# Two attention layers: every other step of the second layer in three products, its exponentials kept in PSUM and its differences taken on GpSimd

## The chip, the cores and the metric

The kernel runs on one core of one Trainium2 chip. The metric is the device time in microseconds (us) of one execution. The kernel before took 3224.03 us as the median of three runs (3221.72 to 3226.51). The execution that was profiled took 3222.18 us, with a span of 3220.4 us from its first to its last instruction. PE is TensorE, DVE VectorE, ACT ScalarE, POOL GpSimd and SP SyncE.

## The reference, cut to what matters

Two attention layers run one after the other on x of shape (4, 64, 64, 256) in fp32: 4 batches of 4096 tokens with 256 channels. A query or key has 32 channels; a value has 256 in the first layer and 128 in the second.

```python
# layer 0
q, k, v = x @ Wq + bq, x @ Wk + bk, x @ Wv + bv
attn = softmax(einsum('bnd,bmd->bnm', q, k), axis=-1)
x = gamma * einsum('bnm,bmc->bnc', attn, v) + x
# layer 1
f, g, v = x @ Wf + bf, x @ Wg + bg, x @ Wh + bh
beta = softmax(einsum('bqd,bkd->bqk', g, f), axis=-1)
x = x + (einsum('bqk,bkd->bqd', beta, v) @ Wo + bo)
```

## The kernel before, in words

No maximum is subtracted in the softmax: `fast_path` takes exp of the raw scores, and a slower general path runs only where sums or values leave a safe range. What is described here is `fast_path`.

**Tiling.** A step (`Step`, line 489) multiplies 1024 exponentials per partition with values. In the first layer (l = 0) a step covers 512 keys for 256 queries, with 8 steps per query block and 16 query blocks per batch. In the second layer (l = 1) a step covers 256 keys for 512 queries, with 16 steps per query block and 8 query blocks per batch. The loop over `steps` (line 654) runs batch by batch, first layer and then second.

**Precision.** In the trace a TensorE matmul of fp32 stands as two records and one of the rounded type fp32r as one. A product of two fp32 matrices can be put together from three fp32r products: rounded parts "high" of both, "low" of both, and differences "d" of both. That is a *split* step: six fp32r matmuls of 512 columns in the second layer. A *plain* step is two fp32 matmuls of 512 columns. Before, all first-layer steps are split, and of the 16 steps of a second-layer block three (i = 2, 7, 12; line 248).

**A step's work.** `scores` (line 498) is issued two steps ahead of the products: TensorE writes the 1024 scores into the PSUM tile `st` (two banks, one buffer). ScalarE reads them and writes exp, as `p`; in a split step it writes exp with a slightly lower bias, rounded, as `high` before it. `cut_low` (line 519), one step ahead, takes low = p - high on VectorE. `cut_both` (line 524) takes d from low and high on VectorE. `products_second` (line 544) adds to two accumulators in PSUM, one bank each, in the order high, low, d. VectorE adds every `p` of the second layer into `p_sum` (line 698), which gives the softmax's denominator.

**Side work.** Between the steps stand *units*: projections of the tokens of the next layer or batch (`project_units`, line 405: transposes, q and k in fp32r parts, v), in blocks of 512 tokens spread over a query block's steps (lines 700 to 705), and the ends of the query block before: `end_first` (line 566) and `end_second` (line 607: evacuate the accumulators, multiply by Wo, divide by the sums, add the residual, store).

**Memory.** [...] `st` 2, accumulators 4 (`ps_acc`), side work 2. In the second layer two of the accumulator banks belong to the current block and two to the one before. GpSimd has small additions (lines 593 and 676) and issues the loads of q and k (line 472), four per block.

**Order.** The source order is not that of the engines: the framework sorts the instructions[...].

## Time and profile before

| what | us or share | where from |
|---|---|---|
| span of the profiled execution | 3220.4 | page |
| time of the profiled execution | 3222.18 | times |
| median of the runs | 3224.03 | times |
| TensorE busy (granted clock 0.998) | 3166.5 (98%) | page |
| VectorE busy | 2691.5 (84%) | page |
| ScalarE busy | 1988.8 (62%) | page |
| GpSimd busy | 661.3 (21%) | page |
| idle before TensorE's matmuls, whole span | 45.9 | sum over the trace |
| layer 1 of batches 0, 1, 2: first to last product | 340.8 | trace, 518.5 to 859.3 and so on |
| layer 1 of batch 3, with no next batch to project for | 301.8 | trace, 2903.1 to 3204.9 |
| a second-layer query block, batches 0 to 2 | 41.7 | trace, starts of consecutive blocks |
| a second-layer query block, batch 3 | 37.2 | trace, 3013.3 to 3050.5 |

A matmul's duration in the trace [...]overlaps the next one's, so sums of durations exceed the time; the pitch is read from consecutive starts. An fp32 matmul of 512 columns stands as two records.

### The profile page before, as it was taken

Reading aid. Unit: us, or ns where it says so; the run is one execution under the profiler, and the core shown is the slowest. Engines: PE = TensorE matmul, PEld = TensorE weight load, DVE = VectorE, ACT = ScalarE, POOL = GpSimd, SP = SyncE. Lnnn points to the kernel's source line nnn. Section 1 sums busy time; section 2 is a strip of 40 time slices with the busy share of each in tenths; the row PEclk is TensorE's granted clock in tenths of the full one; section 3 lists DMA queues with packets and bytes.
Section 4 is the critical chain, followed back from the end, with each engine's and each line's share of the span. In section 5 each row is a group of like instructions: output and inputs, shape, how many; then the busy total and the mean of one; then the engine's idle time right before and its main releaser. Section 6 shows DMA issues by size and latency. Waiting matters only on the chain. (4 is left out here: it accounts for less than half of the span.)

```text
span 3220.4 us, 51144 instructions
## 1 busy us (share of the span) xinstructions
PE 3166.5 (98%) x19460; PEld 2613.0 (81%) x19460; DVE 2691.5 (84%) x3181; ACT 1988.8 (62%) x2483; POOL 661.3 (21%) x784
## 2 busy tenths in 40 slices
PE   8999999999999999999999999999999999999998
PEld 7999997566799999655679999966558999995554
DVE  7888888888888888788888888878888888887776
ACT  6666666655566666565556666655555666665554
POOL 3222223000232222200022222310002222241000
PEclk9999999999999999999999999999999999999999
DMA  4111123221212112322121112232222211121110
GB/s 120 47 47 44 50 50 83 56 53 49 59 44 54 44 52 49 79 53 53 49 64 42 49 50 50 61 70 52 51 52 57 53 41 47 46 70 47 36 36 31
DMA packets 368653, 172.16 MB, mean 53 GB/s; under 512 B 257392, under 2 KB 343664, under 8 KB 368400
## 3 DMA queue, kind: packets, MB, share of 16 engines
q1 hardware_dynamic: 342528, 134.29, 16.0%
q0 software_dynamic: 24960, 34.18, 4.5%
q8 instruction: 157, 2.57, 0.3%
q14 instruction: 96, 0.79, 0.1%
q10 hardware_dynamic: 912, 0.33, 0.0%
HBM read 99.22 MB, written 67.11 MB: 52 GB/s over the span
## 5 line engine op out<-in xcount | busy, mean ns | idle before, releaser
L517 ACT ACTIVATE p<-st 128x1024 f32<-128x1024 f32 x1024 | 1044.5, 1020 | 393.6 <-PE st L505 369.5
L515 ACT ACTIVATE high<-st,down 128x1024 fp32r<-128x1024 f32 x608 | 678.8, 1116 | 683.6 <-PE st L505 572.7
L527 DVE SCALAR_TENSOR_TENSOR d<-low,high 128x1024 fp32r<-128x1024 f32 x608 | 761.2, 1252 | 208.3 <-PE acc L536 202.9
L522 DVE TENSOR_TENSOR low<-p,high 128x1024 fp32r<-128x1024 f32 x608 | 810.6, 1333 | 134.2 <-ACT p L517 134.2
L557 PE MATMUL acc<-p,v 128*128 128x512 f32 x1664 | 795.2, 597 | 0.0
L505 PE MATMUL st<-q,k 128*128 128x256 f32 (+1 forms) x3072 | 778.6, 361 | 8.4 <-ACT p L517 8.3
L698 DVE TENSOR_TENSOR p_sum<-p_sum,p 128x1024 f32<-128x1024 f32 x480 | 587.1, 1223 | 60.7 <-ACT p L517 47.5
L505 PEld LDWEIGHTS st<-q,k 128*128 128x128 f32 x3072 | 461.2, 189 | 210.7 <-ACT p L517 113.3
L536 PE MATMUL acc<-v0d,d 128*128 128x258 f32 x4096 | 591.7, 284 | 1.7 <-DVE d L527 1.6
L536 PE MATMUL acc<-v0h,high 128*128 128x258 f32 x4096 | 588.6, 283 | 1.6 <-ACT high L515 1.6
L536 PE MATMUL acc<-v0l,low 128*128 128x258 f32 x4096 | 587.0, 283 | 0.5 <-DVE low L522 0.5
L536 PEld LDWEIGHTS acc<-v0d,d 128*128 128x128 f32 x4096 | 533.1, 189 | 6.7 <-DVE d L527 3.6
L536 PEld LDWEIGHTS acc<-v0h,high 128*128 128x128 f32 x4096 | 534.1, 190 | 3.4 <-ACT high L515 2.0
L536 PEld LDWEIGHTS acc<-v0l,low 128*128 128x128 f32 x4096 | 532.7, 189 | 0.8 <-DVE low L522 0.7
L557 PEld LDWEIGHTS acc<-p,v 128*128 128x128 f32 x1664 | 308.4, 190 | 214.3 <-issue 184.7
L593 POOL TENSOR_TENSOR x_res<-x,bo 128x256 f32<-128x256 f32 x128 | 216.3, 1690 | 889.9 <-DVE g L583 482.0
L472 POOL DMA_DIRECT2D q<-qk_dram x252 | 123.9, 501 | 1166.1 <-PE st L505 1143.0
L676 POOL TENSOR_TENSOR x_res<-x_res,bv 128x256 f32<-128x256 f32 x128 | 189.6, 1482 | 114.4 <-DMA x_res<-in_x 85.0
L442 PE MATMUL psv<-wv,xT 128*128 128x128 f32 (+1 forms) x1024 | 194.8, 331 | 6.8 <-DVE qk L423 6.1
L442 PEld LDWEIGHTS psv<-wv,xT 128*128 128x128 f32 x1024 | 159.6, 192 | 29.8 <-DVE qk L423 8.5
L472 POOL DMA_DIRECT2D k<-qk_dram x224 | 109.6, 500 | 245.2 <-PE st L505 140.3
L388 DVE TENSOR_TENSOR xl<-xT,xh 128x512 fp32r<-128x512 f32 x128 | 87.1, 683 | 5.1 <-ACT xh L387 4.7
(96 smaller groups left out, 1701.9 us busy)
## 6 DMA issues: line engine op xcount, KB each, us to landing
x_res<-in_x SPq DMA_DIRECT2D x128, 128.0 KB, 2.2
qk_dram<-qk_parts SPq DMA_DIRECT2D x64, 256.0 KB, 2.1
x_dram<-x SPq DMA_DIRECT2D x128, 128.0 KB, 1.7
x_res<-x_res SPq DMA_DIRECT2D x128, 128.0 KB, 1.7
squares<-x_dram SPq DMA_DIRECT2D x256, 64.0 KB, 2.3
x_old<-x_res SPq DMA_DIRECT2D x128, 128.0 KB, 2.0
out<-x_old SPq DMA_DIRECT2D x128, 128.0 KB, 1.7
q<-qk_dram POOLq DMA_DIRECT2D x252, 64.0 KB, 2.1
```

The costliest lines, as they stand in the source:

```text
L442: nc.tensor.matmul(ps[:, t, :], xT[key][:, c, (t0 + t) * P : (t0 + t + 1) * P], wv[l][:, c, :], start=(c == 0), stop=(c == NCC - 1),)
L472: nc.gpsimd.dma_start(dst[n * D : (n + 1) * D, :], parts[h, which])
L505: nc.tensor.matmul(st[:, g, :], k_t[b, l, kt // NT][:, kt % NT * P : (kt % NT + 1) * P], q_t[b, l, j * n // QB][:, q0 : q0 + n], start=Tru ...
L515: nc.scalar.activation(self.high, s_flat, AF.Exp, bias=down)
L517: nc.scalar.activation(self.p, s_flat, AF.Exp)
L522: nc.vector.tensor_sub(self.low, self.p, self.high.bitcast(F32))
L527: nc.vector.scalar_tensor_tensor(self.d, self.low.bitcast(F32), -1.0 / EPS, self.high.bitcast(F32), ALU.mult, ALU.add)
L536: nc.tensor.matmul(acc[2 * s + which][:, :W], p[:, g * QB0 + s * P : g * QB0 + (s + 1) * P], v0[self.i][v][:, g, :], start=self.first and ...
L557: nc.tensor.matmul(acc[which], v[:, g, :], p[:, g * QB : (g + 1) * QB], start=first and g == 0, stop=last and g == G[1] - 1,)
L593: nc.gpsimd.tensor_add(x_old[s], x_new[s], bo_sb)
L676: nc.gpsimd.tensor_add(x_res[b, j][t], x_res[b, j][t], bv)
L698: nc.vector.tensor_add(p_sum, p_sum, s.p)
```

## The change

Eight of the 16 steps of a second-layer block are split (all odd i), where three were. In such a step p is not written to SBUF: ScalarE overwrites the scores in PSUM with it. `high` is scaled down by 2^12 through its bias, so that low = p - 2^12 high is one VectorE instruction with one operand in PSUM and one in SBUF, and d = high - low is taken on GpSimd. Values and Wo are scaled to fit. `p_sum` is divided: VectorE adds the split steps and i = 4, 8, 12; GpSimd adds i = 0, 2, 6, 10, 14 into a second sum of 512 columns, in halves, and one more VectorE addition joins them.

PSUM's accumulators become two pairs of banks. In the second layer the pair that is not accumulating holds scores: steps i = 0, 1, 4, 5, ... use `st`, steps 2, 3, 6, 7, ... the other pair. In step 0 of a block the scores of step 2 are issued after the products, since that pair is the accumulator of the block before. `p` has two buffers instead of three.

Projections go in half blocks of 256 tokens at fixed steps (`plan`): of the next batch one half every 7 steps (transposes at step n, q and k at n + 2, v at n + 3), of the second layer one half per first-layer block.

```diff
+SPLIT1 = (1, 3, 5, 7, 9, 11, 13, 15)
+POOL_SUMS = (0, 2, 6, 10, 14)
...
-    split = [[l == 0 or i % 5 == 2 for i in range(NI[l])] for l in range(2)]
+    NH = N // QB0
+    split = [[l == 0 or i in SPLIT1 for i in range(NI[l])] for l in range(2)]
...
-    ps_st = ctx.enter_context(tc.tile_pool(name="ps_st", bufs=1, space=bass.MemoryType.PSUM))
-    ps_acc = ctx.enter_context(tc.tile_pool(name="ps_acc", bufs=4, space=bass.MemoryType.PSUM))
+    ps_main = ctx.enter_context(tc.tile_pool(name="ps_main", bufs=1, space=bass.MemoryType.PSUM))
...
-        return work.tile([P, 2 * QB], dtype, tag=tag, bufs={"d": 1, "p": 3}.get(tag, 2), name=name)
+        return work.tile([P, 2 * QB], dtype, tag=tag, bufs={"d": 1}.get(tag, 2), name=name)
...
-            st = ps_st.tile([P, G[l], n], F32, tag="st", name=f"st_{self.key}")
+            tag = "st" if l == 0 or i // 2 % 2 == 0 else f"pair{(j + 1) % 2}"
+            st = ps_main.tile([P, G[l], n], F32, tag=tag, name=f"st_{self.key}")
...
-                nc.scalar.activation(self.high, s_flat, AF.Exp, bias=down)
-            self.p = wide("t" if self.split and l == 1 else "p", f"p_{self.key}")
+                nc.scalar.activation(self.high, s_flat, AF.Exp, bias=(down, down1)[l])
+            self.p = s_flat if self.split and l == 1 else wide("p", f"p_{self.key}")
             nc.scalar.activation(self.p, s_flat, AF.Exp)
...
-                nc.vector.tensor_sub(self.low, self.p, self.high.bitcast(F32))
+                if self.l == 0:
+                    nc.vector.tensor_sub(self.low, self.p, self.high.bitcast(F32))
+                else:
+                    nc.vector.scalar_tensor_tensor(
+                        self.low, self.high.bitcast(F32), -UP, self.p, ALU.mult, ALU.add
+                    )
+                    self.d = wide("l", f"d_{self.key}", F32R)
+                    nc.gpsimd.tensor_sub(self.d, self.high.bitcast(F32), self.low.bitcast(F32))
...
+        def add_up(self, sums):
+            on_vector, on_pool = sums
+            if self.l == 0:
+                return
+            if self.i in POOL_SUMS:
+                for part in range(2):
+                    p = self.p[:, part * QB : (part + 1) * QB]
+                    if self.i != POOL_SUMS[0]:
+                        nc.gpsimd.tensor_add(on_pool, on_pool, p)
+                    elif part == 0:
+                        nc.gpsimd.tensor_add(on_pool, p, self.p[:, QB:])
+            elif self.i == 1:
+                nc.vector.tensor_copy(on_vector, self.p)
+            else:
+                nc.vector.tensor_add(on_vector, on_vector, self.p)
...
+    def plan(b, l, j, ends):
+        units = {}
+        def put(i, *some):
+            units.setdefault(i, []).extend(some)
+        if l == 0:
+            if j >= 2:
+                t, qk, v = project_units(b, 1, j - 2)
+                put(0, t), put(4, qk), put(5, v)
...
+        if b + 1 < B:
+            for h in range(NH):
+                i = 10 + 7 * h - j * NI[1]
+                for n, u in zip((0, 2, 3), project_units(b + 1, 0, h)):
+                    if 0 <= i + n < NI[1]:
+                        put(i + n, u)
+        return units
...
         if l == 1:
-            later.scores()
+            if not s.first:
+                later.scores()
             run(todo)
             s.products_second(acc)
+            if s.first:
+                later.scores()
```

## The prediction, on record before the changed kernel ran

> **What bounds the kernel now.** I read the busy table first, then the waits and the window of one second-layer block, then its instructions in order of time. The table says that TensorE is the bound:

> ```profile
> PE 3166.5 (98%) x19460; PEld 2613.0 (81%) x19460; DVE 2691.5 (84%) x3181; ACT 1988.8 (62%) x2483; POOL 661.3 (21%) x784
> ```

> TensorE's own waits in batch 3's whole second layer are short: 6.3 us in 302.

> ```profile
> PE acc L557 <- DVE d L527: 3.7, 8, 1.5
> PE st L505 <- ACT p L517: 2.6, 4, 1.1
> ```

> The timeline of plain steps gives their pitch. Score starts 3015.67, 3017.85 and 3020.03 are 2.18 us apart. From a score's start (3013.89) to the next product's (3014.36) is 0.47: that is the price of two fp32r matmuls of 512 columns. A plain product is the rest, 1.71.

> ```profile
> 3013.89 0.63 PE L505 MATMUL st<-q,k 128*128 128x512 f32 x2
> 3014.36 1.88 PE L557 MATMUL acc<-p,v 128*128 128x512 f32 x4
> 3015.67 1.03 PE L505 MATMUL st<-q,k 128*128 128x512 f32 x2
> ...
> 3017.85 1.03 PE L505 MATMUL st<-q,k 128*128 128x512 f32 x2
> ...
> 3020.03 1.03 PE L505 MATMUL st<-q,k 128*128 128x512 f32 x2
> ```

> A split step's chain, at another place (its scores stream from 529.95, when the product before them is through; their record starts earlier):

> ```profile
> 529.55 1.04 PE L505 MATMUL st<-q,k 128*128 128x512 f32 x2
> ...
> 530.62 1.11 ACT L515 ACTIVATE high<-st,down 128x1024 fp32r<-128x1024 f32 x1 [1.17 <-PE st L505]
> ...
> 531.63 1.02 ACT L517 ACTIVATE p<-st 128x1024 f32<-128x1024 f32 x1
> ...
> 532.68 1.23 DVE L522 TENSOR_TENSOR low<-p,high 128x1024 fp32r<-128x1024 f32 x1 [1.78 <-ACT p L517]
> ```

> So low is ready 533.91 - 529.95 = 3.96 us after its scores begin. Last, GpSimd's additions of 128x256, one alone and one beside VectorE's additions:

> ```profile
> 2659.89 0.74 POOL L676 TENSOR_TENSOR x_res<-x_res,bv 128x256 f32<-128x256 f32 x1 [2.40 <-DMA x_res<-in_x]
> ...
> 2112.18 2.77 POOL L593 TENSOR_TENSOR x_res<-x,bo 128x256 f32<-128x256 f32 x1 [3.50 <-DVE x L585]
> ```

> All 128 of L593 range from 720 to 2772 ns. A quarter of the new size takes 0.72 to 0.74 us even alone.

> [...] L593 above waited behind two VectorE additions, and L698, with a median of 1221 ns, reaches 1753 beside such work. [...]

> **The change part by part.**

> *Removed.* Five steps per block turn from plain to split: 1.71 against six fp32r products, 3 x 0.47 = 1.41. That saves 5 x 0.30 = 1.5 us per block, 32 x 1.5 = 48 us in all, if nothing waits. Work of TensorE in a block of batch 3: 8 x 2.18 + 8 x 1.88 = 32.5, plus 2.1 of outputs (four times 0.43 for 256 fp32 columns and 0.1 for the sums) = 34.6. Before: 13 x 2.18 + 3 x 1.88 + 2.1 = 36.1, measured 37.2.

> *VectorE and ScalarE.* VectorE's low now has an operand in PSUM. Rows with and without one (L402 675, L403 688 ns) show no difference: 1.22 taken, bounds -0.05 and +0.05. ScalarE's p into PSUM: L464, PSUM to PSUM, takes 385 ns against 372 for L463 to SBUF: 1.02 kept. VectorE's three lows, three d, 15 additions and a copy (3 x 1.22 + 3 x 1.22 + 15 x 1.22 + 0.75 = 26.4 us per block) become eight lows, ten additions, a copy from PSUM and a join (18 x 1.22 + 1.1 + 0.7 = 23.8). It isn't the bound.

> *Added on GpSimd.* Eight differences of 1024 and nine additions of 512 per block. [...] Bounds: from below, if what is above 256 elements ran at VectorE's slope (L698, 1221 ns for 1024, against L614, 415 ns for 256: 1.05 ns per element), 1.53 and 0.99; from above, if all were proportional, 2.9 and 1.44. Sum 8 x 2.34 + 9 x 1.26 = 30 us, and 2.0 for the four q loads (496 ns each): GpSimd is nearly as loaded as TensorE[...].

> *The new wait.* From scores to d: 3.96 + 0.08 (semaphore, as between L585 and L593) + 2.34 + 0.05 = 6.43 us. TensorE has between them the scores, the split product before, scores, a plain product, scores, and high and low: 0.47 + 1.41 + 0.47 + 1.71 + 0.47 + 0.94 = 5.47. It is short by 0.96, shared by two successive split steps. Before, d was VectorE's and there were three per block.

> I laid one block of batch 3 (j = 4) out on the engine orders of the built program with these durations. TensorE's waits:
> - d of step 1: behind d of the last block's step 15. 1.4 us.
> - The block's start: scores of steps 2 and 3 come only after d of step 1, since their banks are the accumulator being evacuated. Then two plain exps, high, p (four times about 1.02), low 1.22, d 2.34 stand in a row. Low is 0.8 late, d another 2.0, an output 0.4: 3.2 us.
> - Step 7: 0.9, the shortfall.
> - Step 9: GpSimd's list has half of the sum of step 10 before d of step 9. That p is finished 1.75 us after d of step 7 was consumed; 1.75 + 1.26 + 2.34 + 0.05 = 5.40 against TensorE's 3.6: 1.8 us.
> - Step 13: the same with the sum of step 14, 1.9 us.
> - Steps 5, 11, 15: nothing, the waits before gave them time.

> Sum 9.2; the block takes 34.6 + 9.2 = 43.8 against 37.2: +6.6, eight times +53 us.

> Batches 0 to 2: units fill part of the gaps. TensorE's work is 34.6 + 2.3 half projections x 2.2 (eight records of L442, 1.7, and q and k 0.5) = 39.6. Laid out for block 4 of batch 1: start 2.2; step 9 with both halves of the sum before its d, 2.9; step 15, behind the q loads and behind low, which VectorE reaches only after a half projection's six instructions, 1.9; steps 1, 7, 13 about 0, as v products fill them. Sum 7.0, so 46.6 against 41.7: +4.9, [...] +5.2, 24 times +125 us. In the last block of each batch the k loads add 32 x 0.5 = 16 us to GpSimd's list; about 3 us of that reach TensorE, three times +9.

> *First layer.* Its three products, their order and banks stay. Half projections cost ScalarE and VectorE more: two instructions of 256 columns (385 ns, as L613) for one of 512 (584, as L422), four such per 512 tokens, so 4 x 0.19 = 0.8 us, spread over 16 steps and beside TensorE's products: nothing, and 0.8 us per 512 tokens at most if that cover is gone; 3 us in all for the start, from -3 to +10. With the third p buffer gone, low frees its buffer two steps ahead: nothing.

> Sum: 3222 + 53 + 125 + 9 + 3 = 3412. The median lies 1.9 above the profiled execution; I say 3412.

> **The rivals.**

> *A: the difference arrives in time (faster).* Point of decision: a difference under about 1.1 us, where 3.96 + 0.13 + 1.1 = 5.2 lies inside 5.47. Then of the waits only some 1.8 us at a block's start stay in batch 3 (34.6 + 1.8 = 36.4, -0.8) and 1.0 in the others (40.6, -1.1): 8 x 0.8 + 24 x 1.1 = 33 us less, 3190. For it: the 720 ns could be mostly fixed cost, and no 1024-wide instruction of GpSimd was seen. Against it: a VectorE addition beside a 256-wide one was held up for 1753 - 1221 = 532 ns, so most of the 720 grows with size.

> *B: partly hidden (slower by less).* With 1.53 and 0.99 the same layouts give waits of 4.7 in batch 3 (39.3 - 37.2 = +2.1) and 4.1 in the others (43.7 - 41.7 = +2.0): 8 x 2.1 + 24 x 2.0 = 65, 3287. For it: units may fill more than in the block I laid out.

> *C: GpSimd becomes the bound.* At 2.9 and 1.44: 23 + 13 + 2 = 38 us per block[...]. Waits rise by 3 us per block: 32 x 3 = 96, 3508. [...]

> **How the numbers follow.** Forecast (3310 to 3480) 0.67, B 0.11, C 0.07, A 0.12, and 0.03 for no change, which lies between A and B. 0.2% (6.4 us) is about what a measurement here can tell from no change. Slower 0.67 + 0.11 + 0.07 = 0.85, same 0.03, faster 0.12. The range, 3240 to 3490, reaches past B for the unknown filling by units and up to near C; it leaves out A, no change and most of C.

> **What would show it.** Right: GpSimd's difference near 2.3 us and its addition near 1.3; TensorE's waits led by "acc <- POOL d", with 200 to 300 us in all; second-layer blocks of 44 (batch 3) and 46 to 47; TensorE's busy share near 90%; the first layer at 453 us per batch as before. Wrong: a difference of 1.1 us or less, or d waits that are rare; then the time is below 3222. If blocks last over 50 us with GpSimd at 95%, it is C.

## The result, and the profile after

After the change the kernel takes 3583.39 us (median of four runs, 3579.96 to 3585.72) against 3224.26 for the kernel before beside it: a ratio of 1.111, with a 95% interval from 1.109 to 1.113. The forecast was 3412, with a range up to 3490. The direction was right, and the size was not: of 363 us between the two profiled spans (3583.6 - 3220.4) the forecast had 190.

The busy line of the page, in the same order as before:

```profile
PE 3245.6 (91%) x20036; PEld 2736.7 (76%) x20036; DVE 2831.4 (79%) x3287; ACT 2154.9 (60%) x2771; POOL 1592.1 (44%) x1364
```

No engine is at its bound any more: TensorE fell from 98% to 91%, and GpSimd, the engine with the new work, is at 44%. These shares are averages over both layers; in batch 3's second layer alone TensorE is busy for 302.78 of 377 us (80%) and GpSimd for 260.48 (69%), by a window shown further down. With no engine full, the kernel is held by waits in a chain or a loop. Which ones TensorE sees, over the whole span (us in total, times, longest):

```profile
PE acc L598 <- POOL d L546: 236.9, 166, 3.4
PE st L521 <- ACT p L534: 18.2, 22, 1.6
PE acc L598 <- DVE low L542: 13.9, 17, 1.5
```

The first line is the one that the prediction named, at the size that it named (200 to 300). GpSimd's two kinds of instruction (groups of after: busy us, mean ns, idle before them and what ended it) are also as priced, 2.34 and 1.26 us, though these two prices were my estimates and no trace of before shows them: the medians are 2372 ns for the difference and 1286 for an addition of 512.

```profile
L546 POOL TENSOR_TENSOR d<-high,low 128x1024 fp32r<-128x1024 f32 x256 | 622.5, 2432 | 190.5 <-DVE low L542 162.4 <-PE acc L598 15.7 <-PE psv L450 4.9
L564 POOL TENSOR_TENSOR p_sum_pool<-p_sum_pool,p 128x512 f32<-128x512 f32 x256 | 340.2, 1329 | 284.9 <-ACT p L534 277.9
```

Beside them some of VectorE's instructions last longer. The sums of p_sum and p, both in SBUF, have a median of 2295 ns in after where they overlap an addition or difference of GpSimd (71 of 96), with a longest of 4185, and of 1212 where they don't (25). The lows, with high in SBUF and p in PSUM, have 1220 beside one and 1221 away from it, and never more than 1223. The expectations call this hold-up a lock.

One batch-3 block in time, TensorE's timeline (start, us; the idle time before it and its releaser in brackets):

```profile
3373.94 0.74 PE L598 MATMUL acc<-d,v 128*128 128x512 f32 x2 [1.26 <-POOL d L546]
...
3379.04 0.73 PE L598 MATMUL acc<-d,v 128*128 128x512 f32 x2 [1.16 <-POOL d L546]
...
3386.64 0.73 PE L598 MATMUL acc<-low,v 128*128 128x512 f32 x2 [0.68 <-DVE low L542]
3389.07 1.22 PE L598 MATMUL acc<-d,v 128*128 128x512 f32 x2 [1.70 <-POOL d L546]
3390.08 1.06 PE L521 MATMUL st<-q,k 128*128 128x512 f32 x2
3390.94 2.49 PE L598 MATMUL acc<-p,v 128*128 128x512 f32 x4
...
3394.64 0.62 PE L598 MATMUL acc<-d,v 128*128 128x512 f32 x2
3395.09 0.62 PE L521 MATMUL st<-q,k 128*128 128x512 f32 x2
3395.55 1.88 PE L598 MATMUL acc<-p,v 128*128 128x512 f32 x4
...
3399.90 0.73 PE L598 MATMUL acc<-d,v 128*128 128x512 f32 x2 [1.08 <-POOL d L546]
...
3405.96 0.73 PE L598 MATMUL acc<-d,v 128*128 128x512 f32 x2 [1.75 <-POOL d L546]
...
3416.14 0.73 PE L598 MATMUL acc<-d,v 128*128 128x512 f32 x2 [1.86 <-POOL d L546]
```

The first line is the d product of step 15 of the block before. The others are the d products of steps 1, 3, 5 (no wait), 7, 9 and 13, with the low product of step 3 at 3386.64. Scores that stand behind a waiting d product start after it (3390.08 after 3389.07). The waits are those that the prediction laid out, nearly one by one: 1.16 at step 1 (1.4), 2.38 at the block's start (3.2), 1.08 at step 7 (0.9), 1.75 at step 9 (1.8), 1.86 at step 13 (1.9). Missing there was the one of 1.26 us at step 15.

The timeline also shows what no step of the prediction had. From 3389.07 the matmuls take longer than elsewhere: 1.22 us where a d product that has waited takes 0.73, 2.49 where a plain product takes 1.88. TensorE's granted clock is 0.5 there, from 3388.8 for 3.413 us. The trace's clock record has 133 us at half clock in the second layer of after, against 7 in before.

Where the 363 us are (second layer: from a batch's first product of exponentials with values to its last, four batches; first layer: what lies before and between, the start included):

| us | before | after | difference |
|---|---|---|---|
| start and first layers | 1877.5 | 1944.7 | +67.2 |
| second layers | 1327.5 | 1618.5 | +291.0 |
| after the last product | 15.5 | 20.2 | +4.7 |

(Before, the four second layers last 340.8, 342.4, 342.5 and 301.8 us; the table ahead of the prediction gives the first for three batches.)

### The profile page after: what moved, and what is told of

The parts are those of the page before. It is cut to its first block, busy times and chain, and to the rows that moved or that the text cites. A ratio compares the mean times of both kernels' runs of the same rounds, so it can differ in the third digit from the quotient of the medians.

```text
span 3583.6 us, 54509 instructions
## 1 busy us (share of the span) xinstructions
PE 3245.6 (91%) x20036; PEld 2736.7 (76%) x20036; DVE 2831.4 (79%) x3287; ACT 2154.9 (60%) x2771; POOL 1592.1 (44%) x1364
## 4 chain that ended last, share of the span: by engine, by line
PE 64%; POOL 13%; DVE 9%; ACT 5%; issue 5%; DVEq 0%; DMA 0%; POOLq 0%; ACTq 0%
PE acc L577 41%; PE st L521 11%; POOL d L546 9%; PE acc L598 8%; POOL p_sum_pool L564 3%; DVE low L542 3%; PE psv L450 2%; ACT st L534 2%; DVE p_sum L570 2%; ACT p L534 2%; DVE sums L657 1%; ACT high L531 1%; PE psqk L421 1%; PE pso L666 1%; DVE qk_parts L434 1%
## 5 line engine op out<-in xcount | busy, mean ns | idle before, releaser
L531 ACT ACTIVATE high<-st,down 128x1024 fp32r<-128x1024 f32 x768 | 857.2, 1116 | 875.3 <-PE st L521 680.2
L534 ACT ACTIVATE p<-st 128x1024 f32<-128x1024 f32 x768 | 780.5, 1019 | 308.1 <-PE st L521 306.9
L546 POOL TENSOR_TENSOR d<-high,low 128x1024 fp32r<-128x1024 f32 x256 | 622.5, 2432 | 190.5 <-DVE low L542 162.4
L540 DVE TENSOR_TENSOR low<-p,high 128x1024 fp32r<-128x1024 f32 x512 | 675.7, 1320 | 8.6 <-ACT p L534 8.6
L542 DVE SCALAR_TENSOR_TENSOR low<-high,st 128x1024 fp32r<-128x1024 f32 x256 | 311.3, 1216 | 304.2 <-POOL d L546 140.5
L598 PE MATMUL acc<-p,v 128*128 128x512 f32 x1024 | 518.6, 630 | 3.6 <-DVE o L614 3.6
L564 POOL TENSOR_TENSOR p_sum_pool<-p_sum_pool,p 128x512 f32<-128x512 f32 x256 | 340.2, 1329 | 284.9 <-ACT p L534 277.9
L598 PE MATMUL acc<-d,v 128*128 128x512 f32 x512 | 189.5, 453 | 237.5 <-POOL d L546 236.9
L570 DVE TENSOR_TENSOR p_sum<-p_sum,st 128x1024 f32<-128x1024 f32 x224 | 271.5, 1212 | 0.1
L534 ACT ACTIVATE st<-st 128x1024 f32<-128x1024 f32 x256 | 260.2, 1016 | 0.1
```

The source lines that it names most:

```text
L531: nc.scalar.activation(self.high, s_flat, AF.Exp, bias=(down, down1)[l])
L534: nc.scalar.activation(self.p, s_flat, AF.Exp)
L540: nc.vector.tensor_sub(self.low, self.p, self.high.bitcast(F32))
L542: nc.vector.scalar_tensor_tensor(self.low, self.high.bitcast(F32), -UP, self.p, ALU.mult, ALU.add)
L546: nc.gpsimd.tensor_sub(self.d, self.high.bitcast(F32), self.low.bitcast(F32))
L564: nc.gpsimd.tensor_add(on_pool, on_pool, p)
```

## The experiments

All runs, with the mean length of a second-layer block in batches 0 to 2 and in batch 3 (from one addition of the two halves of `p_sum` to the next, seven intervals each), and the time at half clock in the second layer. Each is one timed execution, except before, after and the last row, which are medians of four or more.

| run | us | first layers | second layers | block, 0-2 | block, 3 | at half clock |
|---|---|---|---|---|---|---|
| before | 3224.3 | 1877.5 | 1327.5 | 41.5 | 37.0 | 7 |
| after | 3583.4 | 1944.7 | 1618.5 | 51.7 | 46.8 | 133 |
| d on VectorE | 3396.0 | 1945.7 | 1428.4 | 46.2 | 40.1 | 10 |
| sums on VectorE | 3447.3 | 1941.5 | 1482.9 | 46.5 | 44.6 | 61 |
| filler matmuls | 3544.4 | 1944.2 | 1579.0 | 50.9 | 44.8 | 27 |
| half-block frame alone | 3258.9 | 1929.2 | 1308.8 | 41.7 | 37.8 | 0 |
| frame, two buffers | 3249.5 | 1920.6 | 1307.8 | 41.7 | 37.8 | 0 |
| d product later | 3486.3 | 1947.7 | 1513.8 | 48.8 | 41.9 | 96 |
| later, three buffers, six splits | 3375.4 | 1935.7 | 1418.5 | 45.0 | 42.3 | 14 |
| no difference | 3214.3 | 1936.8 | 1255.3 | 40.3 | 35.9 | 0 |
| difference unread | 3468.7 | 1957.2 | 1486.0 | 48.1 | 42.3 | 120 |
| difference of high, unread | 3305.8 | 1954.3 | 1329.5 | 42.2 | 36.8 | 27 |
| unread, sums on VectorE | 3410.2 | 1946.5 | 1439.8 | 46.1 | 41.7 | 31 |
| whole blocks, four splits | 3334.2 | 1953.1 | 1362.6 | 42.1 | 40.7 | 3 |

My theory at the start was that d comes after its window (a chain of 6.43 us against 5.47), and that the half clock follows from these waits. Its rivals were GpSimd's throughput and locks, the half-block projections as the main cost, and a half clock that does no harm.

### Who takes the difference, and who the sums

```diff
-                    nc.gpsimd.tensor_sub(self.d, ...)
+                    nc.vector.tensor_sub(self.d, ...)
```

> The difference d is taken on VectorE, right behind low, instead of on GpSimd; all else is as after. Theory T (d comes after its window because of GpSimd's 2.37 us and its place in GpSimd's list): the chain from scores to d falls from 6.43 to about 5.2 us, under the window of 5.47, so the waits on d, 237 us at the d product in the trace of after, fall under 60, the windows of half clock that such waits set off become fewer than 20 (44 in after), and the time is 3380 to 3450, with VectorE at 85 to 90% of the span. Rival 'half-block projections are the main cost': within 30 us of after, 3555 to 3590. Rival 'VectorE becomes the bound': batch-3 blocks longer than 44 us with VectorE over 95% there.

Measured: 3396, 187 us less, in the range of the theory. The half-block projections are not the main cost. But the waits on d stayed at 82.7 us, more than the 60 expected, and the window of batch 0's second layer (us, then busy time of TensorE, its weight loads, VectorE, ScalarE and GpSimd) shows the next limit:

```profile
557.00:924.00 367.00, 334.54 (x1220) 211.76 (x1218) 357.69 (x411) 237.29 (x309) 134.30 (x141) 1.00 0.22 54
```

VectorE is busy for 357.69 of 367 us. In batches 0 to 2 it has no room for eight differences per block; in batch 3 it is not full.

```diff
-POOL_SUMS = (0, 2, 6, 10, 14)
+POOL_SUMS = ()
```

> The partial sums of exponentials of steps 0, 2, 6, 10 and 14 go from GpSimd to VectorE; GpSimd keeps only the differences. Theory T as the prediction laid it out: the waits at steps 9 and 13 (1.8 and 1.9 us of the 9.2 of a block), which are there because sums stand ahead of d in GpSimd's list, vanish; the shortfall of 0.96 us of the steady chain and the block start stay. 2 to 4 us per block are saved, 32 blocks: 3455 to 3520. Rival C (GpSimd and its locks set the pace): more than 4 us per block, under 3450. Rival 'VectorE has no room': no gain, 3570 or more, with VectorE over 88% of the span.

Measured: 3447, 136 us or 4.2 per block. That is a little more than my layout gave and just inside the range of rival C. The sums cost more than the order in GpSimd's list at steps 9 and 13, and this run does not say how.

### The half clock

```diff
+                if self.split and which == 1 and self.i in FILL:
+                    idle = side_psum(f"idle_{self.key}")
+                    for n in range(FILL[self.i]):
+                        nc.tensor.matmul(idle, self.v_h[:, 0, :], self.high[:, :QB], start=True, stop=True)
```

> Ahead of the d products of steps 1, 3, 9 and 13 TensorE repeats 3, 5, 5 and 4 matmuls of the high product into a bank that nobody reads (0.235 us each, 4.0 us per block), so that it works where it waited for d; the output is the same. If the half clock that waits set off is a cost of its own (44 windows of 3.413 us in after, up to 1.7 us each): fewer than 15 windows are left and the time falls by 30 to 70 us, to 3510 to 3555, though TensorE has more to do. If the half clock is harmless (it falls on time that TensorE would wait in any case): no gain, 3575 to 3640, since each matmul that outlasts its wait is added.

Measured: 3544, 39 us less with 544 matmuls more (128 us of streaming at 0.235). The windows of batch 3's second layer, after and then this run (after the busy times: TensorE's clock, DMA share, GB/s):

```profile
3186.00:3563.00 377.00, 302.78 (x1013) 189.50 (x1012) 251.47 (x251) 197.83 (x210) 260.48 (x165) 0.96 0.10 29
```

```profile
3158.00:3523.00 365.00, 327.17 (x1162) 207.83 (x1161) 253.68 (x254) 200.53 (x217) 262.62 (x165) 1.00 0.10 30
```

The clock goes from 0.96 to 1.00, and the second layers get shorter though TensorE does more: from 1618.5 to 1579.0 us, which is the whole gain. So the half clock costs time of its own: at least 39 us, and at most half of the 133 us, 67. It comes with the waits, but not with every wait: with d on VectorE TensorE waits for d for 82.7 us in all and is at half clock for 10. In these runs it goes with how much of one window of 3.413 us the waits fill; the last section has the count.

### The frame alone

The second layer's steps of before, their three buffers for p included, with everything else of after:

```diff
-SPLIT1 = (1, 3, 5, 7, 9, 11, 13, 15)
-POOL_SUMS = (0, 2, 6, 10, 14)
+SPLIT1 = (2, 7, 12)
+POOL_SUMS = ()
...
-            tag = "st" if l == 0 or i // 2 % 2 == 0 else f"pair{(j + 1) % 2}"
-            st = ps_main.tile([P, G[l], n], F32, tag=tag, name=f"st_{self.key}")
+            st = ps_main.tile([P, G[l], n], F32, tag="st", name=f"st_{self.key}")
```

> The frame of after (half-block projections, the plan of units, first-layer accumulators in pairs of banks, loads of half blocks) with the second layer's steps as before: three split steps with their exponentials in SBUF, differences and sums on VectorE, scores in the one pair of banks. The prediction put this frame at +12 us (k loads 9, first layer 3): about 3227 to 3240. Reading of after's trace: the first layer and the start are 68 us longer there than before, and this comes from the frame: 3280 to 3310, with the first query block near 90 us (66 before) and the first layer of a later batch near 464 (453 before). Second-layer stage within 5 us of the 340.8 of before in batches 0 to 2.

Measured: 3259, between the two. The first layers did grow, by 51.7 us, of which 30.6 before the second layer first starts (549.1 against 518.5) and 7 in each later batch. I had not expected that the second layers would get shorter, by 18.7. They hold the same projections as before (144 matmuls of `psv` per batch in both, 16 in batch 3); of the 18.7 us, 15.6 are shorter recorded waits of TensorE there (13.3 us in all against 28.9). From a batch's first second-layer product to the next batch's, both kernels take the same (794.4, 795.0 and 794.4 us here, 793.8, 795.3 and 795.5 before). So the 7 us per later first layer come back in the second layers, and the frame's cost is that of the start, with some 7 us in the last batch and after it.

```diff
-            xT[key] = data.tile([P, NCC, QB0], F32, tag="xT", ...)
+            xT[key] = data.tile([P, NCC, QB0], F32, tag="xT", bufs=2, ...)
...
-                work.tile([P, NCC, QB0], F32R, tag=f"x{what}", bufs=1, ...)
+                work.tile([P, NCC, QB0], F32R, tag=f"x{what}", bufs=2, ...)
...
-            run([u[0] for u in early[:1]])
+            run([u[0] for u in early])
```

> As the run with the half-block frame alone (3258.9), but xT, xh and xl have two buffers and the transposes of both halves of a step of the first query block are issued ahead of the step's later scores, as the whole block's were before. If the 31 us by which the start grew (549 against 518 to the second layer's first product) come from the second half's transposes and copies that queue behind the first half's projection: at least 15 us are won back, 3230 to 3245. If they come from the smaller instructions themselves (more records, more fixed costs): 3254 to 3262.

Measured: 3249.5, 9.4 us less, between the two. Of these 7.6 lie at the start (541.5 against 549.1). So the single buffers and the order of the transposes, which this run changes together, are a quarter of the start's loss of 30.6. What the rest is stays open.

### A later d product

```diff
-            s.products_second(acc)
+            s.products_second(acc, (0, 1, 2) if s.last or not s.split else (0, 1))
+            if held is not None:
+                held.products_second(acc, (2,))
+            held = s if s.split and not s.last else None
```

> As after, d still on GpSimd, but TensorE issues the d product of a split step (all but step 15) only behind the plain product of the next step. The window between a split step's scores and its d product grows by one plain step, from 5.47 to 5.47 + 2.18 = 7.65 us, which is more than the chain of 6.43. Theory T (latency, not throughput): the waits on d fall from 237 us to under 60, half-clock windows from 44 to under 15, a second-layer block to 42 to 44 us in batches 0 to 2 and 37 to 40 in batch 3, the whole to 3270 to 3340 with GpSimd as busy in us as in after. Rival C (GpSimd's throughput and the locks set the pace): a later place in TensorE's order gives GpSimd no time, so 3500 or more. In between would say that the waits behind sums in GpSimd's list are longer than one plain step.

Measured: 3486. My theory missed: with 2.18 us more of window only 97 us came back. TensorE's direct waits on d fell to 61.3 us, but the waits further up did not (this run, VectorE's and GpSimd's waits):

```profile
DVE low L542 <- POOL d L546: 137.7, 76, 2.8
```

```profile
POOL d L546 <- PE acc L600: 29.7, 17, 4.6
```

VectorE's low waits for GpSimd's d. It doesn't read d; both come from one pool of two buffers, in turn low, d, low, d. The low of a split step takes the buffer of the low before it, which GpSimd must first have read. That is a closed loop: low, difference, low of the next split step.

```diff
-SPLIT1 = (1, 3, 5, 7, 9, 11, 13, 15)
+SPLIT1 = (1, 3, 5, 9, 11, 13)
...
-        return work.tile([P, 2 * QB], dtype, tag=tag, bufs={"d": 1}.get(tag, 2), name=name)
+        return work.tile([P, 2 * QB], dtype, tag=tag, bufs={"d": 1, "l": 3}.get(tag, 2), name=name)
```

> As the run with the d product one step later (3486), with three buffers for low and d instead of two, and six split steps (1, 3, 5, 9, 11, 13) instead of eight to make room for the third. In that run VectorE's low waited 138 us for GpSimd's d, whose input low gives the buffer, and GpSimd's d waited 30 us for the d product; low came late, then the sums over p in PSUM, then the scores that need that bank (40 us). If the two buffers are what bound it: TensorE's waits on d, low and p_sum in the second layer fall from 143 to under 50 us, blocks of 38 to 39.5 us in batch 3 and 42 to 44 in the others, 3270 to 3340. If GpSimd's throughput and its list bound it: six eighths of the differences bring it down in proportion only, 3400 to 3440.

Measured: 3375, in neither range. The waits on d, low and p_sum did fall, from 143 to 39 us, but a new one leads (TensorE's and ScalarE's waits in this run):

```profile
PE st L521 <- ACT p L534: 69.6, 52, 2.7
```

```profile
ACT p L534 <- POOL p_sum_pool L564: 129.9, 38, 5.7
```

ScalarE can't write the next plain p, because GpSimd's sum still reads the buffer; scores and then TensorE stand behind it. With one loop open, the next resource that GpSimd holds is the limit.

### Taking the cost apart

Four runs keep TensorE's instructions as in after, all 20036 with their sizes, and change only what stands behind d. (The framework sorts each program anew; TensorE's order differs from that of after at 2.5 to 5.9% of the places.) First no difference at all:

```diff
-                    self.d = wide("l", f"d_{self.key}", F32R)
-                    nc.gpsimd.tensor_sub(self.d, self.high.bitcast(F32), self.low.bitcast(F32))
+                    self.d = self.low
```

> The second layer's differences d are left out, and the d product reads low instead (so the second layer's values are not the reference's; TensorE's instructions, their sizes and their order are those of after). GpSimd keeps only the sums. This gives the floor of after without the wait for d. In the run where VectorE took d, a batch-3 block cost TensorE 37.4 us outside its waits, and in that with the half-block frame alone 37.2, while the prediction had 34.6 against 36.1, that is, 1.5 us less for eight split steps than for three. If the saving of 0.30 us per split step is real and the rest were short waits that the modelled ends hide: a batch-3 block of 35 to 36 us, those of batches 0 to 2 of 40 to 41, and 3190 to 3225 in all. If a split step saves TensorE nothing in this place: 37 to 38 and 41.5 to 42.5, and 3250 to 3280.

Measured: 3214.3, 369 us less than after. The page's busy line:

```profile
PE 3138.4 (98%) x20036; PEld 2706.5 (84%) x20036; DVE 2632.5 (82%) x3287; ACT 2148.7 (67%) x2771; POOL 982.4 (31%) x1108
```

TensorE is the bound again. All else in the change, taken together, is worth about 8 us in its favour against the spans of before: -72 in the second layers, +59 in the first, +5 at the end. The saving of the five more split steps is real: 1.1 us per block in batch 3 against before (37.0 - 35.9), and 1.9 against the frame alone (37.8 - 35.9), where 1.5 was predicted.

Then the difference computed but not read by TensorE:

```diff
-                    (self.d, v["d"], 1, self.first, self.last),
+                    (self.low, v["d"], 1, self.first, self.last),
```

> As after, with GpSimd taking every difference d with the same instruction at the same place in its list, but the d product reads low, so that TensorE never waits for d (the second layer's values are not the reference's). What is left of the difference to the run without d (3214.3) is what d costs through GpSimd's list, its locks with VectorE and the two buffers that low and d share: low of a split step gets its buffer only when d of the step before has been read and written. Theory T (TensorE's own wait for d at the d product is the cost): 3220 to 3300, with 8 GpSimd differences per block in place. Rival C (GpSimd's throughput and locks set the pace, and the wait for d only shows it): 3420 or more.

Measured: 3468.7. My theory of the direct wait falls: without it only 115 of the 369 us go, as rival C said. The timeline of this run, VectorE's lows and GpSimd's list:

```profile
3288.20 2.38 POOL L546 TENSOR_TENSOR d<-high,low 128x1024 fp32r<-128x1024 f32 x1 [1.86 <-DVE low L542]
3290.61 1.22 DVE L542 SCALAR_TENSOR_TENSOR low<-high,st 128x1024 fp32r<-128x1024 f32 x1 [1.36 <-POOL d L546]
3291.97 3.23 POOL L546 TENSOR_TENSOR d<-high,low 128x1024 fp32r<-128x1024 f32 x1 [1.40 <-DVE low L542]
3295.17 2.66 POOL L564 TENSOR_TENSOR p_sum_pool<-p_sum_pool,p 128x512 f32<-128x512 f32 x2
3295.24 1.22 DVE L542 SCALAR_TENSOR_TENSOR low<-high,st 128x1024 fp32r<-128x1024 f32 x1 [0.63 <-POOL d L546]
3297.70 1.23 DVE L570 TENSOR_TENSOR p_sum<-p_sum,p 128x1024 f32<-128x1024 f32 x1
3297.79 3.35 POOL L546 TENSOR_TENSOR d<-high,low 128x1024 fp32r<-128x1024 f32 x1
3301.10 1.27 POOL L564 TENSOR_TENSOR p_sum_pool<-p_sum_pool,p 128x512 f32<-128x512 f32 x1
3301.17 1.22 DVE L542 SCALAR_TENSOR_TENSOR low<-high,st 128x1024 fp32r<-128x1024 f32 x1 [2.25 <-POOL d L546]
```

Each low starts 0.03 to 0.04 us after the end of the difference before it, and each difference waits for its low or for the sums that stand ahead of it. Where two sums stand between two differences, as from 3295.17, the turn takes 3301.17 - 3295.24 = 5.93 us for two steps for which TensorE needs 2.18 + 1.88 = 4.06. Part of that is a lock in the other direction, GpSimd's instruction held up by VectorE's: the difference at 3297.79 lasts 3.35 us, 0.97 more than the 2.38 of the one at 3288.20, and VectorE's sum with two SBUF inputs, at 3297.70, has just begun. Without the lock the turn would be 5.93 - 0.97 = 4.96 us, by this estimate, and still too long.

To open the loop and leave GpSimd its load, the difference then takes high twice:

```diff
-                    nc.gpsimd.tensor_sub(self.d, self.high.bitcast(F32), self.low.bitcast(F32))
+                    nc.gpsimd.tensor_sub(self.d, self.high.bitcast(F32), self.high.bitcast(F32))
```

> As the run whose difference is unread (3468.7), but GpSimd's instruction subtracts high from high instead of low from high: same size, same place in its list, same locks with VectorE, output unread (the second layer's values are not the reference's). It doesn't read low any more, so low of the next split step needs not wait for it. In the trace with low as operand, VectorE's lows start 0.03 to 0.04 us after the end of the difference before (3290.61 after 3290.57, 3295.24 after 3295.20, 3301.17 after 3301.14). Theory L (a closed loop low, difference, low of the next split step, by the buffers that low and d share, with GpSimd's sums in its path): 3220 to 3300. Rival C (GpSimd's load and the locks): 3400 or more. In between divides the cost.

Measured: 3305.8, 6 us above what theory L gave and 94 below C. VectorE's wait for the difference, ahead of low, is gone (the run before, then this one):

```profile
DVE low L542 <- POOL d L546: 122.6, 80, 2.6
```

```profile
DVE low L542 <- POOL d L546: 0.8, 1, 0.8
```

Two things besides the loop changed, so some of this gain is not the loop's. With one operand read twice the instruction takes 1899 ns in the median instead of 2389, 0.5 us less. And the place in GpSimd's list is not the same, as the expectation had it: the framework sorted that list anew, and in the second half of a batch-3 block two differences and then two halves of a sum follow one another, where they alternated one by one.

Last, the unread difference with no sums on GpSimd:

```diff
-POOL_SUMS = (0, 2, 6, 10, 14)
+POOL_SUMS = ()
```

> As the run whose difference is unread (3468.7), but all partial sums are on VectorE, so GpSimd's list in the second layer holds the differences and the q and k loads alone. The loop low (1.22), difference (2.38), two handovers (0.1) is then 3.7 us for two steps, under TensorE's 2.18 + 1.88 = 4.06, if nothing else stands in GpSimd's list or ahead of low on VectorE. Theory L with the sums as what makes the loop too long: the waits fall to a fifth, 3230 to 3310. Rival (VectorE's own list: low stands behind sums that are now all there, and behind locks): 3380 or more. For comparison, moving the sums with d read took 136 us off.

Measured: 3410, the rival. The timeline of a steady stretch of this run:

```profile
3239.14 1.21 DVE L542 SCALAR_TENSOR_TENSOR low<-high,st 128x1024 fp32r<-128x1024 f32 x1
3240.27 1.21 DVE L570 TENSOR_TENSOR p_sum<-p_sum,st 128x1024 f32<-128x1024 f32 x1
3240.49 2.39 POOL L546 TENSOR_TENSOR d<-high,low 128x1024 fp32r<-128x1024 f32 x1 [2.36 <-DVE low L542]
3241.59 2.38 DVE L570 TENSOR_TENSOR p_sum<-p_sum,p 128x1024 f32<-128x1024 f32 x1
3243.89 1.21 DVE L542 SCALAR_TENSOR_TENSOR low<-high,st 128x1024 fp32r<-128x1024 f32 x1
```

The sum with both inputs in SBUF (p_sum and p) takes 2.38 us here, where the one with p in PSUM takes 1.21. It is held until GpSimd's difference ends at 3242.88 and ends 1.09 us after that. The next low stands behind it in VectorE's list, and the next difference behind that low. This loop turns in 3243.89 - 3239.14 = 4.75 us, again more than 4.06. This is the lock again: the sum from 3240.27, with p in PSUM, takes its 1.21 us beside the same difference. So the two loops share the link from low to the difference. One closes by the buffer, the other by the lock and VectorE's order, and taking the sums off GpSimd exchanges the first for the second: low waits for the difference for 17.7 us instead of 122.6, and the difference waits for low for 690.5 instead of 171.6.

The steps from after down, each with the runs that bound it:

| what goes | us | from |
|---|---|---|
| TensorE's own wait at the d product | 115 | 3583.4 - 3468.7 |
| the difference's reading of low (the buffer loop), with 0.5 us of its length and the new order of GpSimd's list | 163 | 3468.7 - 3305.8 |
| what is left of eight GpSimd instructions per block: list and locks | 92 | 3305.8 - 3214.3 |

The parts were taken away in this order only, so the split between them holds for it; loss by half clock is inside each. In the run without differences low also has the pool's two buffers to itself, so the last row holds that, too.

### A version meant to beat both

Whole-block projections as in before, the new steps with four splits, d on VectorE from p in PSUM:

```diff
-SPLIT1 = (1, 3, 5, 7, 9, 11, 13, 15)
+SPLIT1 = (3, 7, 11, 13)
...
-                    nc.gpsimd.tensor_sub(self.d, self.high.bitcast(F32), self.low.bitcast(F32))
+                    nc.vector.scalar_tensor_tensor(
+                        self.d, self.high.bitcast(F32), 1.0 + UP, self.p, ALU.mult, ALU.subtract
+                    )
```

> A version meant to beat both: the projections, plan and first layer of before (whole blocks of 512), the second layer's steps of after with exponentials in PSUM and two pairs of banks, but four split steps (3, 7, 11, 13), which is what fits beside whole-block projections, and d on VectorE, taken from high and p in PSUM, so that it has one SBUF operand only. The run without d put a split step's saving at 0.28 us (batches 0 to 2: 41.69 - 40.28 over five) to 0.39 us (batch 3: 37.81 - 35.86 over five). One split step more than before saves 32 times that, 9 to 12 us, if d comes in time on VectorE (chain 3.96 + 1.22 + 0.05 = 5.2 us against 5.47): 3205 to 3216, ratio to before 0.995 to 0.998, second-layer blocks of 36.7 and 41.2. Rival (waits at the start of a block, where scores stand behind the outputs' banks, take it back): 3222 to 3260.

Measured: 3334.2, ratio 1.034 with an interval from 1.032 to 1.036. Both sides of the expectation missed: the first layers grew by 76 us, though their projections were as before, and a batch-3 block is 40.7. ScalarE's timeline there:

```profile
3177.63 1.02 ACT L529 ACTIVATE p<-st 128x1024 f32<-128x1024 f32 x1 [4.37 <-PE acc L594]
3179.30 1.02 ACT L529 ACTIVATE p<-st 128x1024 f32<-128x1024 f32 x1 [0.64 <-PE acc L594]
3180.22 1.11 ACT L527 ACTIVATE high<-st,down 128x1024 fp32r<-128x1024 f32 x1
```

The exp of a plain step waits for the product that reads its buffer, by 198.7 us in 82 waits over the run, where before has no such wait: the new steps leave two buffers for p where before had three. By this reading two suffice where plain and split steps alternate and not where two or three plain steps follow one another; no run gives this version its third buffer back. Why the first layers grew is not settled. The missing buffer alone is not it: a later first layer takes 459 us both in the frame alone, with three, and in the run without differences, with two, against 470 here and 452 before. No version here that takes the differences beats before.

## Why the prediction was right in direction and wrong in size

Two terms of the sum failed. One is TensorE's clock, which the prediction put at full speed throughout without a reason; the other is the first layer with the start, put at 3 us. They are up to 67 and 64 of the 173 us missed.

- **GpSimd's prices: right.** 2.34 and 1.26 predicted by estimate, medians 2372 and 1286 ns. Those of low, of p into PSUM, of TensorE's products and of the join of the two sums (0.7 us, median 692 ns) held too. One price was missing: the addition of the two halves of `p_sum`, which stands just ahead of the join and in both kernels, has two SBUF inputs and goes from 691 ns in the median to 2980 (691 in the run without differences), so it is GpSimd's differences that hold it up. A slip in the reading of the trace changes nothing: of the two VectorE instructions beside L593 at 2112.18 one is a difference d, not an addition; both have two SBUF inputs.
- **The waits in a block: right in sum, in batch 3 partly by luck.** Batch 3: 9.2 predicted, 9.3 measured; batches 0 to 2: 7.0 and 8.1. In the block above the start was put 0.8 us too long, and 1.26 us at step 15 were not foreseen. The reason given for them, a chain of 6.43 against a window of 5.47 and the order of the list, is only the first layer of it. The prediction checked each difference against its reader and not against the next low, which needs its buffer. So the layout gave the right waits for this order of instructions, and would have given a wrong answer for others: the d product one step later, and the difference unread, were both expected to be cured.
- **Failed: no term for the clock.** The page was read at a clock of 0.998 and every duration taken from there. After has 133 us at half clock in the second layers, which is at most 67 us of the error and at least the 39 that the fillers won back. In a block it is at most 1.6 us in batch 3 and 2.4 in the others.
- **Mis-sized: the first layer.** "3 us in all for the start, from -3 to +10" was +67 for start and first layers; the frame alone gives +52, of which 30.6 at the start. The 7 us that each later first layer gains there come back in the second layers. The cover by TensorE's products, which the step relied on, isn't there at the start, where the projections and the first query block take turns. The first query block's accumulators are evacuated at 118.2 us with half blocks alone, 94.0 before, and from the first products on TensorE is busy for 71.6 of 90.7 us, where it was for 61.9 of 67.3. Why is open, but for the quarter that buffers and order won back.
- **Small terms.** TensorE's work in a block is 35.2 us in batch 3 and 40.0 in the others (the run without differences, less its waits), against 34.6 and 39.6. With the waits and the clock at its most, 0.7 and 1.2 us per block are left over that no recorded wait explains: 46.8 - 35.2 - 9.3 - 1.6 in batch 3, 51.7 - 40.0 - 8.1 - 2.4 in the others.

Of the 173 us missed (363 - 190), the second layers hold 104 (291 less the 187 forecast for them), the first layer 64, the end 5. Rival A's condition was not met, but its number was tested: with no d to wait for the kernel takes 3214, not far from its 3190. Rival C's number was nearest to the time, its reason was not: GpSimd is busy for 260 of 377 us in batch 3's second layer, 69%, so its throughput isn't the bound. Its locks are part of it, inside the 92 us and in both loops.

## What to carry to other kernels

When a link of a chain moves to a slower engine, lay out not only producer to consumer but also consumer back to producer: which buffer the next instance needs, who reads it last, and what stands ahead of that reader in its list. A loop through two engines can be too slow with neither full (in batch 3's second layer of after VectorE is busy for 67% and GpSimd for 69%). And once TensorE waits in a steady pattern, its durations can't be taken from a trace in which it hardly waited (1.22 us at half clock for a d product of 0.73): add a term for its clock where the waits fill about half of a window of 3.413 us or more (half clock followed 43 of 103 windows with 1.6 to 1.9 us and all 82 with more), and none where they stay well below (2 of 5479).
